# A graph attention layer on one core: edge attributes in 1 KB runs, halves of even and odd edges, bf16 places, and target rows in three bf16 parts

## The chip, the core and the metric

The kernel runs on one core of a Trainium2 chip. A core has a matrix engine (TensorE, PE in the profile; its weight loads are listed as PEld), a vector engine (VectorE, DVE), a scalar engine (ScalarE, ACT), a general engine (GpSimd, POOL) and a queue engine (SyncE, SP) that only issues transfers here. Each engine works through its own instructions in order and waits on semaphores for the others. The metric is the device time of one execution in microseconds (us); lower is better. The time before is the median of three runs.

## What is computed

Node features x (12,500 x 128) go through a layer norm and a ReLU and then, with residual, through one layer of graph attention over 400,000 edges. The edges are sorted by their target. What matters of the reference:

```python
h = relu(layernorm(x))
msg_src = h @ w_src + b_src
msg_dst = h @ w_dst
message = msg_src[edge_src] + msg_dst[edge_dst]
rad_w = silu(silu(edge_attr @ w1 + b1) @ w2 + b2) @ w3 + b3     # 32 -> 64 -> 64 -> 128
message = message * edge_weight * rad_w
message = message @ w_sep + b_sep                               # 8 heads of 16 + 16
alpha = smooth_leaky_relu(first 16 of each head);  value = last 16 of each head
score = sum over 16 of alpha * alpha_dot
att = softmax of score over the edges of one target
out[target] = sum of value * att
result = x + out @ w_proj + b_proj
```

## The kernel before

A node stage first writes the two tables msg_src and msg_dst to DRAM. Then the edge stage, nearly the whole time, runs in `windows()` and `passes()`. The edges are cut into 800 sections of 500 (SEC); 400 blocks of two sections are worked on, one block per call of `step(k)`. Because the targets are sorted, all edges of a section point into a window of W = 64 consecutive nodes; if one section does not fit, another branch of the program is taken, which these inputs don't need.

For block k the steps are:

- `gather(k)`: POOL issues eight indirect row gathers of the source rows (line 718), 125 rows of 128 values each, into one of four buffers. It is called four blocks ahead, as `gather(k + 4)`, and can start when the transposes of block k have read that buffer.
- `load_e`: SP loads the 32 attributes of each edge, eight loads for eight blocks, in runs of one edge, 128 bytes. `e_T(k)` transposes them on PE (line 728), and `mlp1`, `mlp2` and `mlp3` (lines 736, 744, 758) are the three layers of the small network, with the silus on ACT (lines 739 and 746). Section f of the block uses half f of the rows and columns of block-diagonal weights.
- `mlp3` also forms rad on DVE (line 761): network output plus bias, times the edge weight.
- `load_d` brings the block's targets as 32-bit integers, repeated over 64 partitions for each section, and `one_hot_T` (line 751) compares them with tgt, a table of the node number that stands on each partition in each block. The result is a 64 x 500 matrix of zeros and ones per section.
- `load_md` loads the 64 rows of msg_dst that belong to each section's window. `message` puts the transposed source rows into PSUM (line 770) and adds the target rows by the product of md with the one-hot matrix (line 775), all in fp32. DVE multiplies the sum by rad (mT, line 779).
- `alphas` (lines 783 to 787), `scores` in every second step (line 794), `load_sm` and the `softmax_` functions once in eight blocks.
- With a lag of twelve blocks (LAG), `sums_begin`, `values` (lines 864 and 866) and `sums` (line 875) weigh the values and add up the edges of each node of the window with a second one-hot matrix, made from the place of the edge in its window (loc). ACT copies the sums to ob (line 879).
- `store_win` stores all 128 rows of ob to win, and `store` the first 63 rows of each half to the result table agg. At the end only the first and last row of each window are read back from win, to join nodes that are cut between sections.
- `prep_load` and `prep_make`, once in 16 blocks: load 128 rows of 125 source and target numbers, subtract the section's first target, and transpose both on PE (line 680) into idx, the row numbers for the gathers, and loc, the places.

The order is written out by hand in `step(k)`: SP's transfers first, then the gathers, then the arithmetic of blocks k, k + 1, k + 2, k + 3 and k - 12. Each engine keeps that order. PSUM is fully used: `misc` (scores, sums, transposes of the preparation and of the softmax), `m1`, `p3`, `pa` and `V` have one buffer each, `pm` two.

Of the kernel before, what the change touches and what calls it, by code (L numbers as in the profile page):

```python
# [21 lines left out]
F32 = mybir.dt.float32  # L22
# [31 lines left out]
EP = 8  # L54
# [3 lines left out]
def gnn_kernel(ctx: ExitStack, tc: tile.TileContext, a: dict, out: bass.AP):  # L58
# [19 lines left out]
    win = dram.tile([NS * W, ROW], F32, name="win")  # L78
    base_d = dram.tile([2, NP], I32, name="base_d")
# [65 lines left out]
    with tc.tile_pool(name="node", bufs=2) as np_, tc.tile_pool(name="node1", bufs=1) as n1, \  # L145
# [103 lines left out]
        def ends_and_cuts():  # L249
# [10 lines left out]
            nc.sync.dma_start(out=base_d.rearrange("f k -> (f k)").unsqueeze(0),  # L260
                              in_=base.rearrange("o f k -> o (f k)"))
# [341 lines left out]
    def windows():  # L603
        with tc.tile_pool(name="wk", bufs=1) as kp:
# [19 lines left out]
            tgt = kp.tile([P, NP], F32, name="tgt")  # L624
            far = kp.tile([P, NS], BF16, name="far")
            with tc.tile_pool(name="tg", bufs=1) as gp, tc.tile_pool(name="tg_ps", bufs=1, space=PSUM) as gq:
# [4 lines left out]
                tb = gp.tile([P, NP], I32, name="tb")  # L631
                nc.sync.dma_start(out=tb[0:W, :], in_=base_d[0:1, :].to_broadcast([W, NP]))
                nc.sync.dma_start(out=tb[W:P, :], in_=base_d[1:2, :].to_broadcast([W, NP]))
                row = gp.tile([P, 1], F32, name="row")
                nc.vector.tensor_copy(row, part)
                nc.vector.tensor_scalar(row[W:P, :], part[W:P, :], float(W), None, op0=ALU.subtract)
                nc.vector.tensor_scalar(tgt, tb, row, None, op0=ALU.add)
# [4 lines left out]
            passes(w1b, w2b, w3b, b12, w_s, b_s, tgt, far)  # L642

    def passes(w1b, w2b, w3b, b12, w_s, b_s, tgt, far):
        src_t = src.rearrange("(t p) -> t p", p=T)
        dst_t = dst.rearrange("(t p) -> t p", p=T)
        ea_t = ea.rearrange("(t p) c -> p t c", p=T)
        dst_p = dst.rearrange("(k f e) -> f k e", f=2, e=SEC)
        ew_p = ew.rearrange("(k e) o -> o k e", e=PR)
        with tc.tile_pool(name="wk2", bufs=2) as sp, tc.tile_pool(name="ps", bufs=1, space=PSUM) as pp, \  # L650
# [3 lines left out]
            eTs, h1s, h2s, ohT, mTs, als, S_all, sms, Ps, Pem, pvx, ohs, accs, pms, pas, Ms = (  # L654
                {} for _ in range(16))


            def prep_load(u):
                t0 = u * P
                ri = lp.tile([P, 2, T], I32, name="ri")  # L660
                rb = lp.tile([P, 1], I32, name="rb")
                nc.sync.dma_start(out=ri[:, 0, :], in_=src_t[t0:t0 + P, :])
                nc.sync.dma_start(out=ri[:, 1, :], in_=dst_t[t0:t0 + P, :])
# [3 lines left out]
                with nc.allow_non_contiguous_dma(reason="a word per tile"):  # L667
                    nc.sync.dma_start(out=rb, in_=at)
# [225 lines left out]
            for i in range(8):  # L894
                load_e(0, i)
# [342 lines left out]
```

## Time and profile before

| | |
|---|---|
| median of three runs | 6634.47 us (6613.69 to 6643.2) |
| profiled execution | 6566.2 us, span of the instructions 6564.2 us |
| mean granted clock of TensorE | 0.873 |
| first gather | 215.9 us after the start of the span |
| moved by DMA | 783 MB in 884,920 packets, 527,255 of them under 512 B |

The share of busy time in the profile is an average. A line of the groups gives the code line, the engine, what is written and read, the number of instructions, busy time and mean duration, then the idle time of the engine just before them and what ended it. In the timeline the columns are the start, the duration, the engine, the line, and in brackets the idle time before it and who ended that; instructions of one line are merged, and SPq marks an issue of SP. Ends of matmuls are modelled.

### The profile page before, as it was taken

What the parts mean: (1) busy time and instruction counts of PE and PEld (TensorE: products, weight loads), DVE (VectorE), ACT (ScalarE), POOL (GpSimd) and SP (SyncE); (2) the same over time, 40 slices, a digit from 0 to 9 for tenths busy, and PEclk for the clock granted to TensorE, in tenths of its full rate; (3) what the DMA queues carried; (4) which work ended last, traced back from release to release, by engine and by line L of the source; (5) the groups of instructions that cost most, each with busy time, mean ns of one, the idle gap of its engine ahead of it and who ended that gap; (6) DMA issues with size and microseconds to landing.
All of it is one profiled execution on the core that took longest, in us unless ns stands there. A gap on an engine that the chain in (4) does not pass through costs nothing. (4 is left out here: it accounts for less than half of the span.)

```text
span 6564.2 us, 79188 instructions
## 1 busy us (share of the span) xinstructions
PE 5066.2 (77%) x26490; PEld 2665.6 (41%) x26490; DVE 2887.1 (44%) x5210; ACT 1785.1 (27%) x3797; POOL 3111.5 (47%) x3231
## 2 busy tenths in 40 slices
PE   3477878787878878788788787887887878888774
PEld 2234444444444444444444444444444444444453
DVE  4234444444444444444444444444444444444465
ACT  3122222222222222222222222222222222222221
POOL 0455555455554545544455454454554545545402
PEclk7688898898998989988888898898888989888885
DMA  3454444444444444444444444444444444444423
GB/s 124 135 144 119 124 119 115 125 117 121 121 122 118 121 119 119 124 117 115 123 120 121 119 116 121 122 115 120 121 117 122 119 120 121 124 119 118 114 60 123
DMA packets 884920, 783.25 MB, mean 119 GB/s; under 512 B 527255, under 2 KB 773279, under 8 KB 884250
## 3 DMA queue, kind: packets, MB, share of 16 engines
q1 hardware_dynamic: 778482, 560.72, 31.0%
q0 software_dynamic: 102816, 210.37, 13.6%
q10 hardware_dynamic: 3202, 6.99, 0.3%
q8 instruction: 212, 3.47, 0.2%
q14 instruction: 208, 1.70, 0.1%
HBM read 643.82 MB, written 134.27 MB: 119 GB/s over the span
## 5 line engine op out<-in xcount | busy, mean ns | idle before, releaser
L718 POOL DMA_INDIRECT gs<-t_src,idx x3200 | 3067.4, 959 | 3189.3 <-PE pm L770 1756.2
L787 DVE SCALAR_TENSOR_TENSOR al<-pa,sl 128x500 f32<-128x500 f32 x800 | 542.9, 679 | 1570.9 <-ACT sl L785 1022.1
L761 DVE SCALAR_TENSOR_TENSOR rad<-p,c_fc_b,w_b 128x500 f32<-128x500 f32 x800 | 553.6, 734 | 1389.4 <-PE p L758 1102.0
L783 PE MATMUL pa<-mT,c_w_a 128*128 128x500 f32 x1600 | 833.7, 603 | 256.8 <-DVE mT L779 248.1
L785 ACT ACTIVATE sl<-pa,c_b_a 128x500 f32<-128x500 f32 x800 | 541.4, 677 | 1789.4 <-PE pa L783 626.9
L864 PEld LDWEIGHTS V<-c_w_v,mT 128*125 128x125 f32 x6208 | 741.2, 188 | 634.8 <-issue 337.9
L864 PE MATMUL V<-c_w_v,mT 128*125 128x128 f32 x6208 | 891.3, 286 | 23.2 <-issue 1.1
L794 PE MATMUL misc<-al,w_s 128*32 128x500 f32 x1600 | 365.9, 986 | 539.5 <-ACT ob L879 525.3
L779 DVE TENSOR_TENSOR mT<-pm,rad 128x500 f32<-128x500 f32 x800 | 504.3, 672 | 280.1 <-PE pm L775 252.8
L758 PE MATMUL p<-h,w3b 64*128 64x500 f32 x1600 | 625.5, 870 | 0.0
L770 PEld LDWEIGHTS pm<-ident,gs 125*128 125x128 f32 x3200 | 430.1, 169 | 435.9 <-issue 435.9
L866 DVE TENSOR_TENSOR pvx<-V,Pem 125x512 f32<-125x512 f32 x776 | 528.9, 682 | 44.4 <-PE m L744 26.5
L770 PE MATMUL pm<-ident,gs 125*128 125x125 f32 x3200 | 533.6, 321 | 0.0
L875 PEld LDWEIGHTS misc<-pvx,oh 125*64 125x64 f32 x6400 | 365.5, 137 | 322.4 <-issue 279.7
L875 PE MATMUL misc<-pvx,oh 125*64 125x136 f32 x6400 | 473.0, 287 | 28.2 <-DVE pvx L866 27.6
L783 PEld LDWEIGHTS pa<-mT,c_w_a 128*128 128x128 f32 x1600 | 269.5, 191 | 500.6 <-DVE mT L779 287.4
L775 PE MATMUL pm<-ohT,md 64*128 64x500 f32 x1600 | 471.0, 656 | 0.1
L739 ACT ACTIVATE h<-p,b 128x500 f32<-128x500 f32 x400 | 270.5, 676 | 700.9 <-PE pa L783 157.2
L879 ACT COPY ob<-misc 128x136 f32<-128x136 f32 x400 | 108.7, 272 | 1292.5 <-remote 630.5
L744 PE MATMUL m<-h,w2b 128*128 128x500 f32 x800 | 449.6, 644 | 0.0
L728 PE MATMUL m<-ident,e_t 125*128 125x125 f32 x800 | 187.4, 319 | 204.4 <-ACT h L746 169.8
L746 ACT ACTIVATE h<-m,b 128x500 f32<-128x500 f32 x400 | 270.7, 677 | 223.4 <-PE m L744 55.0
(145 smaller groups left out, 3153.1 us busy)
## 6 DMA issues: line engine op xcount, KB each, us to landing
w_b<-in_edge_weight SPq DMA_DIRECT2D x400, 500.0 KB
d_b<-in_dst SPq DMA_DIRECT2D x400, 250.0 KB
gs<-t_src,idx POOLq DMA_INDIRECT x3200
e_t<-in_edge_attr SPq DMA_DIRECT2D x400, 125.0 KB
sc_d<-Sp SPq DMA_DIRECT2D x200, 250.0 KB
win<-ob SPq DMA_DIRECT2D x400, 68.0 KB
agg<-ob SPq DMA_DIRECT2D x800, 33.5 KB
md<-t_dst SPq DMA_DIRECT2D x800, 32.0 KB
```

The source lines that it names most:

```text
L718: nc.gpsimd.indirect_dma_start(out=gs[:, j, :], out_offset=None, in_=t_src[:, :], in_offset=bass.IndirectOffsetOnAxis(ap=idx[:, t:t + 1], ...
L758: nc.tensor.matmul(p3[:, f, 0:SEC], w3b[s, :], h2s[k][s, :], start=True, stop=True)
L761: nc.vector.scalar_tensor_tensor(rads[f], p3[:, f, 0:SEC], b3, w_g[k][:, f * SEC:(f + 1) * SEC], op0=ALU.add, op1=ALU.mult)
L770: nc.tensor.matmul(pm[f][:, t * T:(t + 1) * T], gs[:T, f * TS + t, :], ident[:T, :T], start=(t == 0), stop=False, is_transpose=True, skip_ ...
L775: nc.tensor.matmul(pm[f], md[k][s, :], ohT[k][s, :], start=False, stop=True, skip_group_check=True)
L779: nc.vector.tensor_mul(mTs[k][:, f * SEC:(f + 1) * SEC], pm[f], rads[f])
L783: nc.tensor.matmul(pa, w_a, mTs[k][:, f * SEC:(f + 1) * SEC], start=True, stop=True)
L785: nc.scalar.activation(sl, pa, AF.Silu, bias=b_a, scale=1.0)
L787: nc.vector.scalar_tensor_tensor(al, pa, 0.25, sl, op0=ALU.mult, op1=ALU.add)
L864: nc.tensor.matmul(V[:, t, :], mTs[c][:, o:o + T], w_v, start=True, stop=True)
L866: nc.vector.tensor_mul(pvx[c][:, f, :, 0:C].rearrange("p t (h k) -> p t h k", h=H), V.rearrange("p t (h k) -> p t h k", h=H), Pem[c // MP] ...
L875: nc.tensor.matmul(acc[f * W:(f + 1) * W, :], ohs[c][:, f * TS + t, :], pvx[c][:, f, t, :], start=(t == 0), stop=(t == TS - 1), skip_group ...
```

## The change

- **Edge attributes.** The edges of a block are dealt out differently: partition p of a block of 1000 edges gets the eight consecutive edges 8p to 8p + 7, which is one run of 1 KB. One load per block replaces the eight strided loads per eight blocks.
- **Even and odd edges.** The two halves of the network are now the even and the odd edges of the block rather than its two sections. The first silu writes its result in the order of the edges, and rad is formed with a stride of two in one tile of 1000 columns.
- **Places.** `prep_make` works on 32 rows of 500 edges instead of 128 rows of 125. Besides idx and loc it stores the places as bf16 in a DRAM table loc_d. `load_d` loads these for four blocks at a time, and `one_hot_T` compares them with the partition's own number; tgt, base_d and their loads are gone.
- **Target rows.** `split_md` makes three bf16 parts of md, whose sum is md: a bf16 copy, the bf16 copy of what is left, and what is left after that; two copies on ACT, two subtractions on DVE, spread over the step before. `message` adds three bf16 products in place of one fp32 product.
- **Window rows.** win holds only the first and last row of each window, stored by two small transfers.

```diff
             def prep_make(u):
-                ri, rb = prep[u]
-                rows = lp.tile([P, 2, T], F32, name="rows", bufs=1)
+                ri = prep[u]
+                rows = lp.tile([32, 2, SEC], F32, name="rows", bufs=1)
...
+                rb = lp.tile([32, SEC], BF16, name="rb", bufs=1)
+                nc.vector.tensor_copy(rb, rows[:, 1, :])
+                at = loc_d[0:1, 16 * u, :]
+                nc.sync.dma_start(out=bass.AP(at.tensor, at.offset, [[SEC, 16], [NP * SEC, 2], [1, SEC]]), in_=rb)
+                pt = pp.tile([T, 2, TS, 32], F32, name="misc")
                 for j in range(2):
-                    nc.tensor.transpose(pt[:, j, :], rows[:, j, :], ident)
+                    for t in range(TS):
+                        nc.tensor.transpose(pt[:, j, t, :], rows[:, j, t * T:(t + 1) * T], ident[:32, :32])
...
-            def load_e(g, i):
...
-                nc.sync.dma_start(out=e_g[g][:, o::8, :],
-                                  in_=ea_t[:, g * 8 * EP + i:(g + 1) * 8 * EP:8, :])
+            def load_e(k):
+                e_g[k] = lp.tile([T, 8 * RAD], F32, name="e_t", bufs=4)
+                nc.sync.dma_start(out=e_g[k], in_=ea_t[k])
             def load_d(g):
-                d_g[g] = lp.tile([P, 2, SEC], I32, name="d_b")
+                d_g[g] = lp.tile([P, 4, SEC], BF16, name="d_b")
...
+            def split_md(k, i):
+                if i == 0:
+                    m3[k] = lp.tile([P, 3, C], BF16, name="m3")
+                    nc.scalar.copy(m3[k][:, 0, :], md[k])
+                elif i == 1:
+                    mr[k] = lp.tile([P, C], F32, name="mr")
+                    nc.vector.tensor_sub(mr[k], md.pop(k), m3[k][:, 0, :])
+                elif i == 2:
+                    nc.scalar.copy(m3[k][:, 1, :], mr[k])
+                else:
+                    nc.vector.tensor_sub(m3[k][:, 2, :], mr.pop(k), m3[k][:, 1, :])
...
-                nc.scalar.activation(h1s[k].rearrange("p (q e) -> p q e", q=2), p1[:, :, 0:2 * T],
+                nc.scalar.activation(h1s[k].rearrange("x (p g q) -> x q g p", g=2, q=2),
+                                     p1[:, :, 0:2 * T].rearrange("x q (g p) -> x q g p", g=2),
                                      AF.Silu, bias=b12[:, 0:1], scale=1.0)
...
-                ohT[k] = sp.tile([P, SEC], F32, name="ohT")
-                nc.vector.tensor_scalar(ohT[k], d_g[k // 2][:, k % 2, :], tgt[:, k:k + 1], None,
+                ohT[k] = sp.tile([P, SEC], BF16, name="ohT")
+                nc.vector.tensor_scalar(ohT[k], d_g[k // 4][:, k % 4, :], row, None,
                                         op0=ALU.is_equal)
...
-                rads = [sp.tile([C, SEC], F32, name="rad", bufs=3) for _ in range(2)]
+                rad = sp.tile([C, PR], F32, name="rad", bufs=1)
                 for f in range(2):
-                    nc.vector.scalar_tensor_tensor(rads[f], p3[:, f, 0:SEC], b3, w_g[k][:, f * SEC:(f + 1) * SEC],
+                    nc.vector.scalar_tensor_tensor(rad[:, f::2], p3[:, f, 0:SEC], b3, w_g[k][:, f::2],
...
-                for f in range(2):
-                    s = slice(f * W, (f + 1) * W)
-                    nc.tensor.matmul(pm[f], md[k][s, :], ohT[k][s, :], start=False, stop=True,
-                                     skip_group_check=True)
+                for j in range(3):
+                    for f in range(2):
+                        s = slice(f * W, (f + 1) * W)
+                        nc.tensor.matmul(pm[f], m3[k][s, j, :], ohT[k][s, :], start=False, stop=(j == 2),
+                                         skip_group_check=True)
...
             def store_win(c):
-                nc.sync.dma_start(out=win[c * P:(c + 1) * P, :], in_=accs[c])
+                for i in range(2):
+                    nc.sync.dma_start(out=win[2 * c:2 * c + 2, i, :], in_=accs[c][i * (W - 1):P:W, :])
...
             def step(k):
...
+                if has(k + 1):
+                    split_md(k + 1, 0)
                 if has(c):
                     sums_begin(c)
                 if has(k):
                     message(k, mlp3(k))
                 if has(c):
                     values(c, 0)
+                if has(k + 1):
+                    split_md(k + 1, 1)
                 if has(k):
                     alphas(k, 0)
+                if has(k + 1):
+                    split_md(k + 1, 2)
                 if has(c):
                     values(c, 1)
...
                     one_hot_T(k + 1)
+                    split_md(k + 1, 3)
```

## The prediction

> **What bounds it now.** I read the page first, for busy shares.
>
> ```profile
> PE 5066.2 (77%) x26490; PEld 2665.6 (41%) x26490; DVE 2887.1 (44%) x5210; ACT 1785.1 (27%) x3797; POOL 3111.5 (47%) x3231
> L718 POOL DMA_INDIRECT gs<-t_src,idx x3200 | 3067.4, 959 | 3189.3 <-PE pm L770 1756.2
> L775 PE MATMUL pm<-ohT,md 64*128 64x500 f32 x1600 | 471.0, 656 | 0.1
> ```
>
> No engine is full, and the chain of waits explains only the last per cent of the span. POOL does nothing but 3200 row gathers, and more than half of its idle time ends when the transposes of line 770 free its buffer. So I went to the timeline in the middle of the run, from the last gather of one run of eight to the first gather of the run after next.
>
> ```profile
> 3001.14 0.94 POOL L718 DMA_INDIRECT gs<-t_src,idx  x1 [0.30 <-issue]
> 3003.91 0.27 ACT L879 COPY ob<-misc 128x136 f32<-128x136 f32 x1 [3.11 <-remote]
> 3004.23 1.90 PE L794 MATMUL misc<-al,w_s 128*32 128x500 f32 x8 [3.52 <-ACT ob L879]
> 3006.06 2.04 PE L758 MATMUL p<-h,w3b 64*128 64x500 f32 x4
> 3008.03 1.93 PE L770 MATMUL pm<-ident,gs 125*128 125x125 f32 x8
> ...
> 3010.23 0.94 POOL L718 DMA_INDIRECT gs<-t_src,idx  x1 [8.16 <-PE pm L770]
> 3016.51 1.15 PE L875 MATMUL misc<-pvx,oh 125*64 125x136 f32 x16
> 3018.96 0.94 POOL L718 DMA_INDIRECT gs<-t_src,idx  x1 [0.30 <-issue]
> 3018.99 1.07 PE L770 MATMUL pm<-ident,gs 125*128 125x125 f32 x8
> 3021.63 0.27 ACT L879 COPY ob<-misc 128x136 f32<-128x136 f32 x1 [4.34 <-PE pm L775]
> 3022.24 0.95 POOL L718 DMA_INDIRECT gs<-t_src,idx  x1 [2.34 <-PE V L864]
> ```
>
> The reader should see three things. A run of eight gathers takes 3018.96 - 3010.23 = 8.73 us from first to last start. PE's sums (L875) are done at 3017.66 and the next transposes (L770) at 3020.06, yet the engines that wait for PE hear of both only at 3021.6, which is 2.67 us after the last gather's start; in the other step the same copy comes at 3003.91, 2.77 us after 3001.14. Whatever holds PE's signals back ends with the run of gathers. And there are two kinds of step. After an even step POOL starts again 0.6 us after the release: 3022.24 - 3010.23 = 12.01 us, set by POOL alone. After an odd step the scores (L794) need the bank that the copy at 3003.91 frees, then come L758 and L770: 6.3 us more, about 18 us in all. Those three run at half clock, since PE has just idled 3.5 us:
>
> ```profile
> 3003.02:3009.85 6.83, 5.62 (x20) 2.25 (x20) 1.38 (x2) 1.44 (x5) 0.00 (x0) 0.50 0.31 84
> ```
>
> (the 0.50 is the granted clock). From POOL's starts over the middle of the loop, a pair of steps takes 30.4 us; 200 pairs are 6080 of the 6564 us. In odd steps PE finished L770 a median 1.85 us sooner than POOL could use it; in a quarter of them under 0.95 us, in one of twenty not at all. That is the slack of the PE chain under a gather run.
>
> **The change, part by part.** The sum is made against the profiled execution, 6566.2 us (span 6564.2); the median of the timed runs, 6634.47, lies 1.0% above it, so I carry the difference over.
>
> *Edge attributes.* 400 loads of 1000 packets of 128 bytes become 400 loads of 125 packets of 1 KB; SP issues as many. The skill's page "DMA: Bandwidth & Descriptors" (Specifications) puts line rate at 512 bytes a packet and more, so by the rule this is the big gain. The trace says that nobody waits: the group's own view and POOL's starts after the last such load show it.
>
> ```profile
> L693 SPq DMA_DIRECT2D e_t<-in_edge_attr x400: 3/516/6930, 210.0 to 6132.2; - x134
>   PE m L728: 14.0, 2
> ...
> 6145.01 0.94 POOL L718 DMA_INDIRECT gs<-t_src,idx  x1 [8.87 <-PE pm L770]
> 6174.84 0.94 POOL L718 DMA_INDIRECT gs<-t_src,idx  x1 [7.72 <-PE pm L770]
> 6205.34 0.94 POOL L718 DMA_INDIRECT gs<-t_src,idx  x1 [6.87 <-PE pm L770]
> 6237.10 0.94 POOL L718 DMA_INDIRECT gs<-t_src,idx  x1 [7.04 <-PE pm L770]
> ```
>
> From 6132.2 on there are no edge loads, and the pairs still take 29.8, 30.5 and 31.8 us. Waiting for them is 14.0 us, all at the start, where eight loads (15.3 us of SP) stand ahead of the first edges' transposes at 226.9; POOL then has a hole of 6.1 us at 255.7 to 261.9, once its first 32 gathers are through. Two loads in place of eight close it: -6 (0 to -10). Gathers that took longer than 942 ns stretch the runs by 17 us in all; I give half of it: -5.
>
> *Places as bf16.* The loads of d_b halve in bytes and number, and the comparison (471 ns, DVE) gets cheaper by 0.2 to 0.3 us. Both lie under the gather run: 0. The table tgt and its two loads go from the start (-1), and the first preparation is 1 us longer (+1).
>
> *Three bf16 parts.* Line 775 is four instructions now (two passes for each of two halves), 1.11 us; it becomes six bf16 ones. The passes of a pair start 0.52 us apart here; the trace has no bf16 product. From below: half that spacing, three pairs end about 0.2 us sooner. From above: six passes one after the other, with weights that don't load under the pass before, at 0.3 us each are 1.8 us, 0.7 more than now. I take the first, because L770's weight loads do hide at 0.105 us each. It lies after L770, under the gather run, so it helps only the fifth of odd steps without slack: 0.2 x 40 = -8; uncovered, 400 x 0.2 = -80.
>
> *Making the parts.* Each step gets two ACT copies and two DVE subtractions of 128x128. Nearest rows: 260 ns (ACT) and 290 ns (DVE) for that size in the node stage, so about 0.55 us per engine and step, 220 us each, on engines that are 27% and 44% busy. Queued behind copy 1 (which waits for md, loaded two steps before): the two copies of L847, then the silu of L785; behind subtraction 1 (waits for copy 1): L787; behind copy 2: the silus of L739 and L746, the second of which the next transposes (L728) wait for; behind subtraction 2: the second L787. ACT sits idle before L739 in most steps, DVE before L787. Cost 0; without cover 0.3 x 400 = +120.
>
> *Halves of even and odd edges.* Same element counts, but L739's output, rad and w_b are strided. For DVE, line 1042 does strided 128x512 multiplies in 681 to 692 ns against 672 for the plain mT: 0. For ACT no row shows a stride of four words; between nothing and twice 0.68 us. I take 0, the DVE row being nearest; a double would eat 0.7 us of slack.
>
> *Window rows.* The store of 128 rows becomes two stores of two rows: one more issue of 0.4 us on SP each step, half of one less for d_b. Behind it on SP stand agg, w_b and md, all needed two steps later: 0.
>
> *Preparation, once in 16 steps.* Two 128-row transposes (L680) become eight of 32 rows. This one is on the path, between the scores and L758, at half clock: L680 starts at 3279.78 and L758 at 3280.49 in one such step. The skill's page "TensorE: Matmul & The Clock Gate" (LDWEIGHTS) speaks against it: the time of a weight load goes by its columns, so 32 rows cost as much as 128. Counting the streamed columns alone (8 x 32 = 2 x 128) the cost would be 0; by the rule, with L770's half-clock pace (8 in 1.93 us; 0.21 each), six more are +1.2; by L680's own 0.36 each, +2.1. I take +1.0, as L770's pace is nearest and part of the wait for ACT's score copy covers some: 25 x 1.0 = +25 (0 to +53). DVE's longer casts (four times the columns, +0.8 us) fall into its idle time before the release, and the added store of places is needed five steps later.
>
> Sum: -6 -5 -8 +25 = +6, so 6572 profiled and **6640 us** against the median.
>
> **Rivals.** (1) *Faster by more, chance 0.20.* Some 24 of the 188 even gaps are over 4.5 us instead of 3.3, about 55 us together; in them the V products' signal came late. If fewer packets, or an L775 that is shorter at half clock, clear them, and the start gives 10 us and the gathers all 17: 6634 + 25 - 55 - 10 - 17 - 8 = about 6570. For it: they gather around steps 0 and 8 of 16. Against: the tail without edge loads has them too (4.04 at 6188.56). (2) *Slower, chance 0.24: the parts use up the slack.* Place: ACT's queue ahead of L746, hence L728 to L770. If copy 2 (0.3), a doubled L739 (0.7) and serial parts (0.7) add up to 1.7 us, the quarter of odd steps with under 0.95 us of slack lose some 1.1 us, the next quarter some 0.3: 200 x 0.36 = +72, with the +6 above 6712. It decides from about 0.9 us on. For it: in the pair above L746 ends at 3016.46, only 1.1 us before L728 starts. Against: the named copies stand in gaps of their engines. (3) *Preparation at its upper end, the rest as forecast, 0.08:* 6670. (4) *The release moves, 0.03:* if the held signals had to do with the fp32 product, odd steps lose up to 2 us: 6300.
>
> **How the numbers follow.** The likeliest case has 0.45, with its own range 6605 to 6672. About 0.5% (33 us) is what a measurement of this kernel can tell from no change. Within it lie nearly all of the likeliest case and a few of the others: same 0.45. Faster: rival 1's greater part, rival 4 and the low edge: 0.23. Slower: rivals 2 and 3 and the high edge: 0.32. The range 6555 to 6725 leaves out rival 4, the far part of 2 and the low tail of 1.
>
> **What would show it.** Right: even steps still 12.0 us from gather run to gather run, pairs at 30 us, L775 at about 0.9 us, no hole in POOL's starts before 262, q1's packets down by 400,000 or more with POOL's pattern unchanged, eight short L680s taking about 1.7 us. Wrong: ACT's copy of ob no longer 2.7 us after the last gather's start; even gaps spread above 3.3 with L728 waiting longer for L746; L739 over 0.68 us; or a granted clock that is no longer half after the idle spell.

## The result and the profile after

| | before | after |
|---|---|---|
| timed runs, median | 6631.22 us (6613.69 to 6643.2, four runs) | 6865.86 us (6838.89 to 6875.8, four runs) |
| ratio | | 1.035, 95% interval 1.0312 to 1.0387 |
| span of the profiled execution | 6564.2 us | 6863.6 us |
| packets, MB moved | 884,920, 783 | 431,585, 706 |
| mean gap between two runs of gathers, after even and after odd steps | 3.69 and 9.17 us | 4.48 and 10.01 us |

The change is 235 us slower where 6 us were forecast; the range ended at 6725 us. A gap is the time from the start of the last gather of a run of eight to the first of the next; the runs themselves stayed at 8.78 us. The profile shown before the prediction was of a quick execution. Another profile of the same kernel (E13 below) has a span of 6639.2 us and gaps of 3.78 and 9.43 us; against that one the changed kernel loses 0.70 + 0.58 = 1.28 us in a pair of steps, 256 us in 200 pairs, and the spans differ by 224: the start is 17 us shorter (first gather of block 16 at 419.5 us, 436.6 in E13).

From the profile of the changed kernel, the busy shares and groups that answer to those shown of before:

```profile
PE 5120.2 (75%) x27440; PEld 2711.2 (40%) x27440; DVE 3055.5 (45%) x6034; ACT 2104.6 (31%) x4597; POOL 3082.9 (45%) x3231
...
L716 POOL DMA_INDIRECT gs<-t_src,idx x3200 | 3038.6, 950 | 3517.7 <-PE pm L770 2135.8 <-issue 831.4 <-PE pm L776 286.2
...
L737 ACT ACTIVATE h<-p,b 128x500 f32<-128x500 f32 x400 | 461.8, 1155 | 1188.6 <-PE misc L877 278.2 <-PE m L743 245.1 <-PE pa L785 236.4
...
L776 PE MATMUL pm<-ohT,m 64*128 64x500 bf16 x2400 | 385.4, 402 | 33.0 <-issue 31.6 <-DVE M L827 0.7 <-DVE M L822 0.3
...
L726 PE MATMUL m<-ident,e_t 125*128 125x125 f32 x800 | 196.7, 333 | 626.3 <-ACT h L745 544.1 <-issue 60.7 <-ACT h L737 17.6
```

ACT does 320 us more than before (2104.6 against 1785.1) and is still busy for only 31%; PE, DVE and POOL do about as much as before. POOL does the same gathers and stands idle 328 us longer (3517.7 against 3189.3). Silu 1 (L737, before L739) takes 1155 ns instead of 676. The edge transposes (L726, before L728) wait 544 us for silu 2 instead of 170 (268 in E13). The edge loads themselves still keep nobody waiting, as the view of their line says (duration in ns: least, median, most):

```profile
L680 SPq DMA_DIRECT2D e_t<-in_edge_attr x400: 3/457/1406, 216.1 to 6539.5; - x134
...
  PE m L726: 3.7, 1
```

A step in the middle, from the timeline (SPq marks an issue of SP):

```profile
3379.88 0.94 POOL L716 DMA_INDIRECT gs<-t_src,idx  x1 [9.62 <-PE pm L770]
...
3383.24 1.71 SPq L696 DMA_DIRECT2D md<-t_dst  x2
...
3385.78 1.19 ACT L737 ACTIVATE h<-p,b 128x500 f32<-128x500 f32 x1 [2.62 <-PE m L743]
...
3388.62 0.95 POOL L716 DMA_INDIRECT gs<-t_src,idx  x1 [0.30 <-issue]
3388.75 0.68 ACT L745 ACTIVATE h<-m,b 128x500 f32<-128x500 f32 x1 [1.79 <-issue]
3389.48 0.20 PEld L726 LDWEIGHTS m<-ident,e_t 125*128 125x128 f32 x2 [2.73 <-ACT h L745]
...
3390.89 1.07 PE L770 MATMUL pm<-ident,gs 125*128 125x125 f32 x8
...
3391.74 0.27 ACT L881 COPY ob<-misc 128x136 f32<-128x136 f32 x1 [0.18 <-PE pm L770]
3392.04 1.07 SPq L886 DMA_DIRECT2D win<-ob  x2
3392.35 1.33 POOL L716 DMA_INDIRECT gs<-t_src,idx  x1 [2.79 <-PE pm L770]
```

The copy of ob still comes about 3 us after the last gather's start (3391.74 - 3388.62). What grew is the lateness of silu 1 and silu 2: silu 1 starts 2.2 us on the mean after its input is ready and ACT is free, 0.8 us in the profile before. So L726 and L770 start late, and POOL waits. SP's line is the one to remember: the issue of md's loads ends at 3384.95, 5.1 us after the first gather.

### The profile page after: what moved, and what is told of

Same layout as the page of the kernel before. It is cut to its first block, busy times and chain, and to the rows that moved or that the text cites. A ratio compares the mean times of both kernels' runs of the same rounds, so it can differ in the third digit from the quotient of the medians.

```text
span 6863.6 us, 83815 instructions
## 1 busy us (share of the span) xinstructions
PE 5120.2 (75%) x27440; PEld 2711.2 (40%) x27440; DVE 3055.5 (45%) x6034; ACT 2104.6 (31%) x4597; POOL 3082.9 (45%) x3231
## 2 busy tenths in 40 slices
DMA packets 431585, 705.90 MB, mean 103 GB/s; under 512 B 109622, under 2 KB 307118, under 8 KB 430888
## 4 chain that ended last, share of the span: by engine, by line
PE 62%; ACT 9%; DVE 9%; another core or an unknown queue 8%; issue 7%; DMA 1%; SPq 1%; ACTq 0%; POOL 0%; DVEq 0%; POOLq 0%
PE V L866 10%; PE pa L785 8%; PE p L758 8%; PE pm L770 7%; PE misc L796 6%; PE misc L877 6%; PE m L743 5%; PE pm L776 4%; PE p L734 3%; PE m L726 3%; ACT h L745 3%; ACT h L737 3%; DVE rad L761 3%; DVE mT L781 2%
## 5 line engine op out<-in xcount | busy, mean ns | idle before, releaser
L716 POOL DMA_INDIRECT gs<-t_src,idx x3200 | 3038.6, 950 | 3517.7 <-PE pm L770 2135.8
L866 PEld LDWEIGHTS V<-c_w_v,mT 128*125 128x125 f32 x6208 | 759.6, 192 | 508.3 <-DVE pvx L868 231.3
L866 PE MATMUL V<-c_w_v,mT 128*125 128x128 f32 x6208 | 907.5, 290 | 24.4 <-issue 4.4
L737 ACT ACTIVATE h<-p,b 128x500 f32<-128x500 f32 x400 | 461.8, 1155 | 1188.6 <-PE misc L877 278.2
L726 PE MATMUL m<-ident,e_t 125*128 125x125 f32 x800 | 196.7, 333 | 626.3 <-ACT h L745 544.1
L796 PE MATMUL misc<-al,w_s 128*32 128x500 f32 x1600 | 415.1, 999 | 329.5 <-ACT ob L881 311.9
L770 PEld LDWEIGHTS pm<-ident,gs 125*128 125x128 f32 x3200 | 434.4, 170 | 443.0 <-issue 441.5
L770 PE MATMUL pm<-ident,gs 125*128 125x125 f32 x3200 | 539.8, 324 | 0.0
L776 PE MATMUL pm<-ohT,m 64*128 64x500 bf16 x2400 | 385.4, 402 | 33.0 <-issue 31.6
L726 PEld LDWEIGHTS m<-ident,e_t 125*128 125x128 f32 x800 | 95.0, 158 | 720.9 <-ACT h L745 613.1
```

What stands on the lines that cost most here:

```text
L716: nc.gpsimd.indirect_dma_start(out=gs[:, j, :], out_offset=None, in_=t_src[:, :], in_offset=bass.IndirectOffsetOnAxis(ap=idx[:, t:t + 1], ...
L737: nc.scalar.activation(h1s[k].rearrange("x (p g q) -> x q g p", g=2, q=2), p1[:, :, 0:2 * T].rearrange("x q (g p) -> x q g p", g=2), AF.Si ...
L770: nc.tensor.matmul(pm[f][:, t * T:(t + 1) * T], gs[:T, f * TS + t, :], ident[:T, :T], start=(t == 0), stop=False, is_transpose=True, skip_ ...
L776: nc.tensor.matmul(pm[f], m3[k][s, j, :], ohT[k][s, :], start=False, stop=(j == 2), skip_group_check=True)
L796: nc.tensor.matmul(ps[32 * j:32 * j + 32, :], w_s, als.pop(2 * k - 2 + j), start=True, stop=True)
L866: nc.tensor.matmul(V[:, t, :], mTs[c][:, o:o + T], w_v, start=True, stop=True)
```

## The experiments

The eighteen runs were made in five sets, each on one chip with its own runs of the kernel before; ratios hold within a set. Sets 3 and 5 are listed on the same chip, number 15. The kernel before took 6532.7, 6644.0, 6642.2, 6644.0 and 4921.5 us in them. The last number is no misprint, and it is taken up at E17. The theories are named in each expectation (Q stands for the slack on ACT up to E6, and for SP's queue from E17 on).

### Set 1: undo one part

**E1**, silu 1 on plain rows, the order made by PE's transposes and by rad on DVE:

```diff
-                    nc.tensor.transpose(pe[:, g, :], ev[:, g, :], ident[:T, :T])
+                    nc.tensor.transpose(pe[:, :, g], ev[:, g, :], ident[:T, :T])
...
-                nc.scalar.activation(h1s[k].rearrange("x (p g q) -> x q g p", g=2, q=2),
-                                     p1[:, :, 0:2 * T].rearrange("x q (g p) -> x q g p", g=2),
+                nc.scalar.activation(h1s[k].rearrange("p (q e) -> p q e", q=2), p1[:, :, 0:2 * T],
...
-                    nc.vector.scalar_tensor_tensor(rad[:, f::2], p3[:, f, 0:SEC], b3, w_g[k][:, f::2],
+                    v = "c (e q f) -> c f q e"
+                    nc.vector.scalar_tensor_tensor(rad.rearrange(v, q=2, f=2)[:, f], ...
```

> The changed kernel, with silu 1 reading and writing plain rows again; the order of the edges is made by the transposes' writes to PSUM (stride 2) and by the strided output of rad on DVE instead. Theory S (the strided write of silu 1, 1155 against 676 ns, on the way L737, L743, L745, L726 is what costs the time): silu 1 falls to about 0.68 us, PE's wait of L726 for L745 from 544 to some 170 us, and of the 232 us that the change costs about 200 go: 6640 to 6700. Theory P (the making of the parts and the six products on the queues): silu 1 falls, the time stays near 6866. Theory V (the preparation with eight transposes): stays near 6866 too. If PE writes with stride 2 slowly or DVE does, the transposes L726 or rad L761 last longer, and the gain is smaller by that.

**E2**, the kernel before with only the strided write:

```diff
-                nc.scalar.activation(h1s[k].rearrange("p (q e) -> p q e", q=2), p1[:, :, 0:2 * T],
+                nc.scalar.activation(h1s[k].rearrange("x (p g q) -> x q g p", g=2, q=2),
+                                     p1[:, :, 0:2 * T].rearrange("x q (g p) -> x q g p", g=2),
```

> The kernel before, with silu 1 alone writing in the strided order (edges within a half come out mixed, so the messages are not those of the reference; no work is left out). Theory S: silu 1 goes from 676 to about 1155 ns and the time by about 200 us, to some 6830. Theories P and V: silu 1 lasts longer, under cover of the gathers, and the time stays at 6631, at most 6660.

**E3**, no three parts:

```diff
-                for j in range(3):
-                    for f in range(2):
-                        s = slice(f * W, (f + 1) * W)
-                        nc.tensor.matmul(pm[f], m3[k][s, j, :], ohT[k][s, :], start=False, stop=(j == 2),
+                for f in range(2):
+                    s = slice(f * W, (f + 1) * W)
+                    nc.tensor.matmul(pm[f], md[k][s, :], ohT[k][s, :], start=False, stop=True,
...
-                if has(k + 1):
-                    split_md(k + 1, 0)
```

> The changed kernel without the three parts: no copies and subtractions, the target rows and the one-hot in fp32, four-pass product as before. Theory P: 100 to 230 us come back, 6640 to 6760. Theory S: the two ACT copies (0.6 us a step) are off the queue ahead of L745, but the strided silu stays: no more than 60 us come back, 6800 to 6870; as on record, the longer product may cost 8 us. Theory V: 6866.

**E4**, two 128-row transposes again:

```diff
-                pt = pp.tile([T, 2, TS, 32], F32, name="misc")
+                pt = pp.tile([T, 2, P], F32, name="misc")
                 for j in range(2):
-                    for t in range(TS):
-                        nc.tensor.transpose(pt[:, j, t, :], rows[:, j, t * T:(t + 1) * T], ident[:32, :32])
+                    nc.tensor.transpose(pt[:, j, :], rows[:, j, :], ident)
```

> The changed kernel with the gather indices and places transposed by two 128-row transposes again (the bf16 places are still stored from rows of 500; three more loads per 16 steps on SP). Theory V: over 100 us come back, below 6760. Theories S and P: only what the gap after the step with the preparation shows (12.6 against 10.4 us there, some 0.7 of it as in other odd steps): 25 x 1.5 = about 40 us, 6825.

| | ratio to before, 95% interval |
|---|---|
| E1 | 1.013 (1.0083 to 1.0177) |
| E2 | 1.0005 (0.9992 to 1.0019) |
| E3 | 1.0112 (1.0069 to 1.0154) |
| E4 | 1.0213 (1.0161 to 1.0264) |

E2 speaks against theory S. Its silu 1 is as slow as in the changed kernel, and nothing follows. The groups of E2 and E1:

```profile
L739 ACT ACTIVATE h<-p,b 128x500 f32<-128x500 f32 x400 | 464.3, 1161 | 659.3 <-PE m L745 142.2 <-PE p L736 122.0 <-PE V L865 102.9
```

```profile
L761 DVE SCALAR_TENSOR_TENSOR rad<-p,c_fc_b,w_b 128x500 f32<-128x500 f32 x800 | 853.9, 1115 | 630.4 <-PE p L757 479.9 <-PE pm L778 103.2 <-PE pm L772 19.5
```

E1 has moved the price rather than removed it: with a stride of four words rad takes 1115 ns instead of 734. The changed kernel was not run in this set, so what E1, E3 and E4 gave back is not known from it. They can only be read as prices of what each still holds; I went on by adding parts to the kernel before.

### Set 2: parts alone and together

**E5** adds `split_md`, the six products and the bf16 one-hot to the kernel before, at the places of the changed kernel:

```diff
+                if has(k + 1):
+                    split_md(k + 1, 0)
                 if has(c):
                     sums_begin(c)
...
-                    nc.tensor.matmul(pm[f], md[k][s, :], ohT[k][s, :], start=False, stop=True,
+                        nc.tensor.matmul(pm[f], m3[k][s, j, :], ohT[k][s, :], start=False, stop=(j == 2),
```

> The kernel before with the three bf16 parts alone: two ACT copies and two subtractions a step at the places of the changed kernel, six bf16 products, a bf16 one-hot; silu 1 plain, edges, places and preparation as before. Theory Q (ACT's queue has room for one of the two additions, 0.6 us of copies or 0.48 us of strided silu, not for both; the slack of rival 2): no slower than 0.4%, ratio 0.997 to 1.004. Theory N (the making of the parts is what costs): ratio 1.015 to 1.025. Theory R (neither; the rest of the change): ratio 1.0.

**E6** is E5 with the edit of E2 as well.

> The same with silu 1 writing in the strided order too (the edges within a half come out mixed; no work is left out). Theory Q: 1.07 us more on ACT a step pass the slack: ratio 1.015 to 1.025, with the wait of the edge transposes for silu 2 at 400 us or more. Theory N: as the parts alone. Theory R: under 1.005; then the eight transposes, the even and odd halves or the loads carry the loss.

**E7** is the changed kernel, unedited.

> The changed kernel once more, on the chip of these runs, as the measure for all the single edits. All theories: ratio 1.031 to 1.039 as in the first measurement. If it is 1.02 here, the single edits above gave back less than they seem to.

**E8** lets silu 1 read PSUM out of order and write plain rows:

```diff
-                nc.scalar.activation(h1s[k].rearrange("x (p g q) -> x q g p", g=2, q=2),
-                                     p1[:, :, 0:2 * T].rearrange("x q (g p) -> x q g p", g=2),
+                nc.scalar.activation(h1s[k].rearrange("x (p g q) -> x p g q", g=2, q=2),
+                                     p1[:, :, 0:2 * T].rearrange("x q (g p) -> x p g q", g=2),
```

> The changed kernel with silu 1 reading PSUM in the permuted order and writing plain rows. If the price lies in the strided write, silu 1 takes about 0.68 us and the time comes to a ratio of 1.005 to 1.015 (the edit with the permutation on DVE gave 1.013 although rad rose by 0.38 us a piece). If ACT pays for any order that is not plain, silu 1 stays at 1.15 us and the ratio at 1.035.

| | ratio | silu 1 |
|---|---|---|
| E5 | 1.0012 (0.999 to 1.0034) | 677 ns |
| E6 | 1.0019 (1.0001 to 1.0037) | 1158 ns |
| E7 | 1.0334 (1.0305 to 1.0364) | 1154 ns |
| E8 | 1.0301 (1.0277 to 1.0325) | 678 ns |

Theory Q falls: both additions on ACT, 0.6 and 0.48 us a step, cost 0.2% together. E8 says the same from the other side, and shows that ACT pays for the strided write only; with the reordering on the PSUM read it takes 678 ns. E8 and E1 do not agree, though: both give silu 1 its plain write back, and one stands at 1.030, the other at 1.013 in another set. No run tells why. E6 fell in an instructive way. Its transposes do wait as the theory wanted,

```profile
L741 PE MATMUL m<-ident,e_t 125*128 125x125 f32 x800 | 189.3, 322 | 458.2 <-ACT h L760 337.9 <-issue 90.2 <-ACT h L752 25.4
```

longer for silu 2 than in either profile of before (169.8 us, and 268.0 in E13), and the time hardly followed: some 400 of its 458 us lie under runs of gathers.

### Set 3: edges and places

**E9** takes only the edge part into the kernel before: `load_e`, `e_T`, the strided silu 1, `mlp3` with one rad tile.

> The kernel before with the edge part alone: loads of 1 KB, halves of even and odd edges, strided silu 1, one rad tile with strided writes; places, product, preparation and window rows as before. Parts and silu alone cost 0.1% and 0.05%, the whole change 3.3%, so something else or a sum carries it. Theory D (the one rad tile: the first multiplication of mT, which needed the first rad only, now waits for both; 0.98 against 0.79 us after the first gather in odd steps): ratio about 1.006 (200 x 0.2 us = 40 us). Theory T (places and preparation carry the rest): ratio 0.998 to 1.003. Theory L (the loads themselves gain): below 0.997.

**E10** takes only places, preparation and window rows: `prep_load`, `prep_make`, `load_d`, row in place of tgt, `store_win`.

> The kernel before with places as bf16 from the stored table, eight transposes of 32 rows in the preparation and the window stores of two rows; edges and product as before. Theory T: ratio 1.005 to 1.012, all of it after the step with the preparation and its neighbours. Theory D: under 1.003. The forecast's own term for it was +25 us, ratio 1.004.

**E11** is E9 with the three parts, **E12** is E10 with the three parts. So that all fits, the tile of the loaded numbers has one buffer in E10 and E12, and mr one in E12.

> Edge part and three bf16 parts together, preparation and places as before. If edge part and parts multiply (PE's held signals move ahead to silu 1 with the parts, and the late mT pushes the odd step's chain into them): ratio 1.015 to 1.025, more than the sum of the two alone by 0.01 or more. If the terms merely add: the sum of the two alone, under 1.010.

> Places, preparation, window stores and three parts together, edges as before. If the terms add: the places alone plus 0.001. If the parts leave no slack and the preparation's lateness now counts in full: more than the sum by 0.005 or more, ratio 1.012 to 1.02.

| | without the parts | with the parts |
|---|---|---|
| edge part | E9: 1.0032 (1.0014 to 1.005) | E11: 1.0081 (1.0053 to 1.0108) |
| places, preparation, window rows | E10: 1.0175 (1.012 to 1.023) | E12: 1.0264 (1.0199 to 1.0329) |

Theory T: the loss sits where the forecast saw nothing but the preparation; it is larger than the theory had (1.005 to 1.012), and E12 lies above what either expectation had. The parts cost 0.1% alone, 0.5% beside the edge part and 0.9% beside the places. The intervals of the last two differences are about 0.3 and 0.9 points, so that the cost of the parts grows is not settled.

### Set 4: which of the three

**E13** is the kernel before, unedited, for its profile.

> The kernel before, unedited, for a profile from the chip of these runs. All theories: its own time. If PE's signals under the gathers come later here than in the first profile of before (in odd steps silu 1 started 0.4 us late on the mean there, 1.3 to 1.6 us in the single edits), then a part of what the profiles of the single edits show belongs to the chip and not to the edit; if it is 0.4 us again, it belongs to the edit.

**E14** changes only the window stores (and where their rows are read back at the end):

```diff
-                nc.sync.dma_start(out=win[c * P:(c + 1) * P, :], in_=accs[c])
+                for i in range(2):
+                    nc.sync.dma_start(out=win[2 * c:2 * c + 2, i, :], in_=accs[c][i * (W - 1):P:W, :])
```

> The kernel before with the window stores of two rows alone (two small stores a step on SP in place of one of 128 rows). Of the ratio of 1.0175 that places, preparation and window rows cost together: theory W (SP is late with the loads behind the second store): 1.008 or more. Theories V (eight transposes) and B (bf16 places): 0.997 to 1.002, as forecast.

**E15** has the bf16 places without window rows and with two transposes:

```diff
+                rb = lp.tile([32, SEC], BF16, name="rb", bufs=1)
+                nc.vector.tensor_scalar(rb, ri, rf, None, op0=ALU.subtract)
...
-                d_g[g] = lp.tile([P, 2, SEC], I32, name="d_b")
+                d_g[g] = lp.tile([P, 4, SEC], BF16, name="d_b")
...
-                nc.vector.tensor_scalar(ohT[k], d_g[k // 2][:, k % 2, :], tgt[:, k:k + 1], None,
+                nc.vector.tensor_scalar(ohT[k], d_g[k // 4][:, k % 4, :], row, None,
```

> The kernel before with the bf16 places (their table stored by the preparation, d_b loaded from it every fourth step, one row vector in place of tgt), but two 128-row transposes and no window rows. Theory B: 1.008 or more. Theory V: under 1.003. Theory W: under 1.003.

**E16** has the eight transposes alone:

```diff
-                    nc.tensor.transpose(pt[:, j, :], rows[:, j, :], ident)
+                    for t in range(TS):
+                        nc.tensor.transpose(pt[:, j, t, :], rows[:, j, t * T:(t + 1) * T], ident[:32, :32])
```

> The kernel before with the preparation from rows of 500 and eight transposes of 32 rows, without bf16 places and window rows (one score tile in place of two makes the room). The preparation's transposes last 1.88 us in place of 0.79, so 25 x 1.1 = 27 us, ratio 1.004, if only PE's time counts (the forecast's +25). Theory V: 1.008 or more, and then it is not PE's time but what stands behind it. Theories B and W: 1.002 to 1.005.

| | ratio | in us of 6644 | mean gap, even and odd |
|---|---|---|---|
| E13, before | | | 3.78, 9.43 |
| E14, window rows | 1.0271 (1.0224 to 1.0318) | +180 (149 to 211) | 4.49, 9.75 |
| E15, places | 0.9998 (0.9978 to 1.0018) | -1 (-15 to +12) | 3.85, 9.32 |
| E16, eight transposes | 1.0048 (1.0029 to 1.0067) | +32 (19 to 45) | 3.84, 9.53 |

The smallest edit of all, a store of four rows in place of 128, carries most of the loss: theory W, as far as it says where. E10, which contains it and the eight transposes, showed less in another set: 1.0175 (1.012 to 1.023), where the two alone come to 3.2% here. Its price is not one fixed number, or the prices do not add.

How it costs shows beside E13, one even step of each. First the kernel before (E13), then E14; in both, PE had finished the second V product 4.4 and 4.6 us and the first layer 5.0 and 5.3 us after the first gather.

```profile
1352.78 0.94 POOL L718 DMA_INDIRECT gs<-t_src,idx  x1 [9.06 <-PE pm L770]
...
1354.05 1.09 SPq L711 DMA_DIRECT2D md<-t_dst  x2
...
1358.49 0.69 DVE L866 TENSOR_TENSOR pvx<-V,Pem 125x512 f32<-125x512 f32 x1 [1.09 <-PE p L736]
...
1359.94 0.68 ACT L739 ACTIVATE h<-p,b 128x500 f32<-128x500 f32 x1 [3.25 <-PE pa L783]
...
1361.52 0.94 POOL L718 DMA_INDIRECT gs<-t_src,idx  x1 [0.30 <-issue]
1362.08 0.43 PE L728 MATMUL m<-ident,e_t 125*128 125x125 f32 x2 [1.34 <-ACT h L746]
...
1363.48 1.07 PE L770 MATMUL pm<-ident,gs 125*128 125x125 f32 x8
...
1364.34 0.27 ACT L879 COPY ob<-misc 128x136 f32<-128x136 f32 x1 [1.75 <-PE pm L770]
...
1364.64 0.35 SPq L883 DMA_DIRECT2D win<-ob  x1
...
1364.95 0.94 POOL L718 DMA_INDIRECT gs<-t_src,idx  x1 [2.49 <-PE pm L770]
```

```profile
2904.51 0.94 POOL L718 DMA_INDIRECT gs<-t_src,idx  x1 [10.32 <-PE pm L770]
...
2906.58 1.30 SPq L711 DMA_DIRECT2D md<-t_dst  x2
...
2912.57 0.69 DVE L866 TENSOR_TENSOR pvx<-V,Pem 125x512 f32<-125x512 f32 x1 [3.18 <-PE pa L783]
...
2913.27 1.20 POOL L718 DMA_INDIRECT gs<-t_src,idx  x1 [0.30 <-issue]
...
2916.13 0.68 ACT L739 ACTIVATE h<-p,b 128x500 f32<-128x500 f32 x1 [7.46 <-remote]
...
2917.43 0.68 PE L728 MATMUL m<-ident,e_t 125*128 125x125 f32 x2 [2.92 <-ACT h L746]
...
2917.83 0.28 ACT L879 COPY ob<-misc 128x136 f32<-128x136 f32 x1
...
2918.14 1.09 SPq L884 DMA_DIRECT2D win<-ob  x2
...
2920.01 1.93 PE L770 MATMUL pm<-ident,gs 125*128 125x125 f32 x8
...
2922.21 0.95 POOL L718 DMA_INDIRECT gs<-t_src,idx  x1 [7.74 <-PE pm L770]
```

Two stores hold SP 1.09 us where one held it 0.35, and they stand ahead of the step's loads. So the issue of md's loads ends 3.37 us after the first gather in the second step, 2.36 in the first. In the second, DVE starts on V only 8.06 us after the first gather, 3.4 us after PE had it done, silu 1 starts after 11.62, and the gap is 8.9 us where it usually is 3.5.

The late signal is not all of it. Below are the sums from the first edge transpose (L728) to the next gather, for E13 and then for E14; the third number from the end is the granted clock of TensorE.

```profile
1362.08:1364.95 2.87, 2.87 (x16) 1.64 (x18) 1.86 (x4) 1.12 (x5) 0.38 (x1) 1.00 0.11 29
```

```profile
2917.43:2922.21 4.78, 4.78 (x16) 2.68 (x18) 2.73 (x5) 1.28 (x5) 0.00 (x1) 0.50 0.11 24
```

PE had idled 2.9 us before L728 in E14, 1.3 in E13. Of the 5.5 us that this gap is longer, 3.6 are L728's later start and 1.9 the slower products behind it. Over the loop, the eight transposes of L770 took more than 1.5 us (1.07 at full clock, 1.93 at half) at the end of 20 of 188 even gaps in E13, and those gaps are 6.3 us on the mean, the others 3.5; in E14 it is 43 of 188, with 7.2 and 3.7 us.

Over the 280 steps in the middle of the loop (the end of the issue of md's second load, counted from the first gather):

| | E13, before | E14, window rows |
|---|---|---|
| median end of md's issues, even and odd steps | 2.39, 4.20 us | 3.38, 5.72 us |
| even steps: mean gap where they end before 3 us | 3.56 us (94 steps) | 3.50 us (42) |
| from 3 to 4 us | 3.68 us (19) | 4.27 us (52) |
| after 4 us | 4.46 us (27) | 5.78 us (46) |

The gap grows with SP's lateness in both kernels, and E14 has moved its steps to the late side. The steps hit hardest fit too: the gaps after steps 0 and 8 of 16 rise from 4.07 and 4.04 to 5.60 and 6.16 us, and just ahead of those SP also waits for the scores that it is to read back. This is a correlation, of steps that share a queue, and neither lateness is enough by itself: in E1 the issues of md end later still (median 4.0 us in even steps) at a mean even gap of 4.0 us, and in E6 silu 1 starts nearly as late as in E14 (1.9 and 2.0 us on the mean) at a cost of 0.2%. Set 5 was to test whether late loads cause late signals.

### Set 5: the place of the stores

**E17** is the changed kernel with its window stores at the end of SP's step:

```diff
                 if has(c - 1):
-                    store_win(c - 1)
                     store(c - 1, 0)
...
                 if has(c - 1):
                     store(c - 1, 1)
+                    store_win(c - 1)
```

> The changed kernel, with the two window stores moved to the end of SP's step, behind the loads of w_b, md, d_b and e_t and the stores of agg; the same stores, the same bytes. Theory Q (the second window store pushes the loads behind it on SP by 0.8 us in even and 1.6 us in odd steps, into the second half of the gather run, and steps whose md loads end later than 4 us after the first gather have gaps of 5 us and more): the md loads end at 2.4 us or earlier in even steps, and the ratio falls from 1.034 to 1.01 or below (silu, parts, edges and eight transposes are left). Theory K (the stores of two rows themselves do it, wherever they stand, by their few packets from two partitions): ratio 1.025 or more.

**E18** is the kernel before with the stores behind the loads:

```diff
-                if has(c - 1):
-                    store_win(c - 1)
-                    store(c - 1, 0)
...
                 if has(c - 1):
+                    store_win(c - 1)
+                    store(c - 1, 0)
                     store(c - 1, 1)
```

> The kernel before, with its window store of 128 rows and the first store of agg behind the loads of the step on SP. Theory Q: the loads end earlier than 2.4 and 4.0 us after the first gather, the few even gaps over 5 us go, and the kernel gets faster, ratio 0.985 to 0.997. Theory K: 1.0. If loads that no longer wait for the sums are then issued under the end of the gather run before, where PE's signals are held, theory Q would give no gain or a loss, up to 1.01.

The kernel before took 4921.5 us in this set (4917.58 to 4925.05, nine runs), 26% less than in all others. E17 took 4814.96 us, ratio 0.978 (0.9766 to 0.9793), and E18 5126.02 us, ratio 1.0419 (1.0405 to 1.0433). The timeline of E17 tells what is missing:

```profile
2372.08 0.94 POOL L716 DMA_INDIRECT gs<-t_src,idx  x1 [0.62 <-PE pm L770]
...
2376.30 1.16 ACT L737 ACTIVATE h<-p,b 128x500 f32<-128x500 f32 x1 [0.95 <-PE p L734]
2376.43 1.07 SPq L886 DMA_DIRECT2D win<-ob  x2
...
2378.06 1.15 PE L877 MATMUL misc<-pvx,oh 125*64 125x136 f32 x16
...
2379.25 0.27 ACT L881 COPY ob<-misc 128x136 f32<-128x136 f32 x1
```

The sums end at 2379.21 and are copied at 2379.25, in the midst of the gathers. No signal of PE is held: silu 1 starts 0.03 us late on the mean (E14: 2.0), and the gaps are 1.28 us after even and 2.17 us after odd steps, against 1.25 us between two gathers of a run. The cure that E17 was to show had nothing to cure here, so Q and K are not told apart. The changed kernel itself was not run in this set either. What stands is that with its window stores behind the loads it beats the kernel before by 2.2% where signals are not held.

E18 missed what both theories expected, it seems by other waits; that these lead to the loss is read from the trace, not shown by a run. Behind the edge loads of 1000 packets the store of 128 rows takes long to issue (median 2282 ns, 423 in E13). Copies of ob wait for a free buffer, DVE's softmax waits 139 us for the scores that SP reads back (S), and POOL waits 681 us for the transposes (225 in E17):

```profile
L883 SPq DMA_DIRECT2D win<-ob x400: 340/2282/8517, 431.9 to 4955.5; - x134
...
POOL gs L718 <- PE pm L770: 680.6, 387, 10.8
...
DVE M L815 <- DMA S<-sc_d: 138.6, 43, 11.7
ACT ob L879 <- DMA agg<-ob: 103.1, 53, 10.7
```

## Why the prediction was wrong

**Window rows, the step that failed.** The prediction wrote: one more issue of 0.4 us on SP each step, behind it agg, w_b and md, "all needed two steps later: 0". Alone this edit measured +180 us (E14). The issue was sized about right (two of 0.51 us for one of 0.42), and no engine waited for md's loads in E14. So that the data behind the stores are needed late was true, and it did not make the cost 0: the issues of md end 1.0 us later in even and 1.5 us later in odd steps, silu 1 starts 2.0 us late on the mean instead of 1.4 (E13), PE then runs at half clock more often, and both gaps grow (by 0.71 and 0.32 us). That the edit costs is shown; whether by the place of the stores on SP (Q) or by the stores themselves (K), and why PE's signals are held at all, stays open.

**The slack.** "Slack of the PE chain under the gather run" was the right thing to look at, but it was measured in one profile, of a quick execution. In E13, the same code, silu 1 hears of its input 1.1 us late in odd steps on the mean, 0.43 in that profile. Even gaps above 3.3 us, which the prediction named as a sign of being wrong, did spread: 54 of 188 are over 4.5 us in the changed kernel, 24 in the profile before.

**Rival 2** had the sign and the manner (signals and parts eat slack until POOL waits) and the wrong place. On ACT ahead of silu 2, 1.07 us more a step cost 0.2% (E6), though it "decides from about 0.9 us on" there. The edit that cost lies on SP's queue.

**Silu 1, L739.** The term was 0, with a doubled duration as the upper end. The duration rose to 1155 ns, so the nearest row, a strided DVE multiplication, was a poor guide, and the cost alone was +3 us (-5 to +12; E2). Right in the sum, wrong in the row.

**Three parts: -8 for the product, 0 for the making.** At full clock six products take 0.81 us where four took 1.11, 0.3 us less where 0.2 was forecast. The parts alone measured +8 us (-7 to +23; E5). The one-hot came 0.06 us cheaper (415 for 478 ns), not 0.2 to 0.3; it mattered as little.

**Preparation: +25.** Eight transposes take 1.88 us instead of 0.78, and E16 measured +32 us (19 to 45). What the Trainium skill, "TensorE: Matmul & The Clock Gate" (LDWEIGHTS), says of weight loads, and the prediction set against counting streamed columns, agrees with the trace: a weight load of 32 rows takes 321 ns (E16), one of 128 rows 304 (E13). Streamed columns alone said 0.

**Edge loads -6, gathers -5, places 0.** The hole after the first 32 gathers is gone, and one of 12.5 us stands after the first 40 instead; by block 16 the gathers are 11 us ahead of the first profile (419.5 us for 430.8). What gathers take beyond 942 ns did fall (54 us in all in the first profile, 44 in E13, 26 after), but the runs of eight are as long as before. The whole edge part, its strided tiles included, cost +21 us (9 to 33; E9) instead of -11. Places: -1 (E15).

Added up, single edits give 180 + 32 + 21 + 8 - 1 = 240 us, near the 235 measured. With E10 in mind (116 us for window rows, places and transposes together, where the single terms say 211) that agreement is in part luck.

## What to carry to other kernels

A queue that only issues transfers has a schedule too: an added issue can cost although nobody waits for the data behind it, as E14 shows, so try it alone. Where the stores should stand is not settled here: E18 moved them behind the loads and lost 4.2%, and E17 has no run beside it with the stores in their old place. Undoing parts needs the changed kernel in the same set; adding parts to the kernel before one at a time gave the answer here. And a slack that a forecast leans on should be taken from more than one execution.

## What the runs showed of the hardware

**Signals of PE that are held are not there in every set.** In four sets they were there; in the fifth they were absent, and the kernel before ran some 1700 us of 6640 shorter. The chip does not explain it, if its number tells: set 3 ran on number 15 too, and the kernel before took 6642 us there. Single instructions of ACT and POOL took as long as ever (silu 2 673 ns in E17, most gathers 0.94 us). TensorE's granted clock was higher, 0.96 and 0.95 on the mean in E17 and E18 against 0.85 to 0.88 in the other profiles, and PE was busy for 92% of E17's span, 75% of the changed kernel's. One more thing differs in the traces: those of E17 and E18 hold 110,407 and 119,280 records of semaphore updates, those of before, E13 and after 45,817, 44,671 and 37,347, for about the same work. In the first 200 us, ahead of all gathers, E13 and E18 hold nearly as many (1121 and 1151); within the runs of gathers E13 holds 5 per us and E18 24. So records were lost where signals were late, and in sets 1 to 4 who ended a wait, which the brackets take from these records, is less sure than when an instruction started. The Trainium skill, "NOTIFIC — the notification-queue block" (section 7.1), says that the block which writes such records can push back on its producers and stall an engine. That fits, but no run here shows it. It would mean that part of what was compared in sets 1 to 4, and of the 235 us, belongs to the recording.

**ACT pays for a strided write, not for the reordered read.** 128x500 fp32: 1155 ns written with a stride of four words, 678 ns when PSUM is read in the permuted order and the write is plain (E8). On DVE a stride of two words was free (734 ns), one of four cost 1115 ns (E1).

**An issue of SP takes long behind a load of many packets.** The store of agg, which stands partly behind the 1000-packet edge load, takes 962 ns on the mean in E13 and 267 ns behind the load of 125 packets (E9). SP's issues together fall from 2343 to 1573 us (E13, E9), and the time did not fall with them: E9 is 0.3% slower than the kernel before. So the rule of 512 bytes a packet, from the Trainium skill, "DMA: Bandwidth & Descriptors" (Specifications), which the prediction had doubted, brought no gain here, where nobody waited for the loads.
